# Expert tiles in a two-layer kernel: 36 instead of 39, the last eight made of two halves of different experts

## The chip, the cores and the metric

The kernel runs on one core of a Trainium2 chip. The time is device time of one execution in microseconds (us); a lower time is better. All data are float32, apart from small 0/1 tables in bfloat16. In the profile PE is TensorE (matmuls and transposes), PEld its weight loads, DVE is VectorE, ACT ScalarE, POOL GpSimd, SP SyncE; L433 is line 433 of the kernel. A float32 matmul that is no transpose shows as two records ("passes") of its row, so four matmuls are counted x8.

## What is computed

Two layers on x of shape (4, 512, 512), which is T = 2048 tokens of 512 numbers. Each layer normalises x and adds an attention and a mixture of experts to it. The first attention has 16 heads of 128 with compressed sparse and windowed local parts, the second is a plain one with 16 heads of 32. The change concerns the experts: 8 of them, and each token goes to the 2 with the highest logits.

```python
def _L0_ffn_ref(x, Wr, We, be):
    logits = jnp.einsum('bsd,de->bse', x, Wr)
    w, sel = jax.lax.top_k(logits, K_TOP)
    w = jax.nn.softmax(w, axis=-1)
    gate = jnp.einsum('bsk,bske->bse', w, jax.nn.one_hot(sel, E, dtype=w.dtype))
    for e in range(E):
        out = out + gate[..., e:e + 1] * (jnp.einsum('bsd,df->bsf', x, We[e]) + be[e])
    return out

def _L1_ffn_ref(...):
    ...
    h = jnp.einsum('td,edf->etf', xf, expert_w) + expert_b[:, None, :]
    expert_out = jax.nn.silu(h)
    combined = jnp.einsum('etf,te->tf', expert_out, full_w.reshape(-1, E)).reshape(B, S, D)
    out = jnp.einsum('bsd,df->bsf', combined, proj_w) + proj_b
    y = x + out
    rms = jnp.sqrt(jnp.mean(y * y, axis=-1, keepdims=True) + EPS)
    return norm_w * (y / rms)

xn = _layernorm(x)
x = x + _L0_attn_ref(xn, ...) + _L0_ffn_ref(xn, ...)
xn = _layernorm(x)
return x + _L1_attn_ref(xn, ...) + _L1_ffn_ref(xn, ...)
```

## The kernel before

**Layer 0's attention** runs as 32 steps (g, b): 8 groups of two heads (HG = 2), 4 sequences each. A step takes about 46 us. It projects queries, keys and values of the *next* step (`first`, `second`, `third`, `fourth`, `fifth`, L604 to L645; their matmuls are L575, and VectorE takes each product out of PSUM, L610, L631, L639), computes scores (L658, L667), turns and applies them (L693, L709 to L714, L727) and projects the result (L742). A group's weights are two blocks, `wA` and `wB`, double-buffered and loaded at the group's first step by `load_group` (L84); `combine_weights` (L107) makes four differences of them at the group's last step but one, for the next group.

**Layer 1's attention** is a walk over 64 places (g, kc): `weights` (scores of four heads, L1137, each on 32 rows of the array) and `attend` (L1151, four heads, each writing 32 columns: PSUM partitions 32 h to 32 h + 31).

**Experts.** The tokens of each expert get *slots*. Each expert's slots are rounded up to whole tiles of 128, so with 4096 token-expert pairs and 8 experts NS = 39 tiles always suffice, and all 39 are computed. Class `Routing` makes the lists. `choose` (L270) picks the two experts and counts. `place` (L306) gets the rank of each token within its expert by three small matmuls into the PSUM tile `rk` (with the triangular tables `tri` and `tri8`), and turns it into `slot` (two per token), and `wrow` (the rows of the weight array in which the weights of each tile's expert lie) by a chain of small VectorE operations (L313 to L349). `mark` and `list` (L353 to L380) invert that into `rows`, the token of each slot.

Class `Experts` (L385) handles tile i:

- `fetch_rows`, `fetch_weights`, `fetch_bias` (all through L398): indirect DMAs issued by GpSimd: the 128 token rows `xr`, the expert's weights `we` and, in layer 1, the bias `be`. In layer 0 the bias is a part of `we` (`fetch`, L413).
- `turn` (L419): four transposes on TensorE into `trm`, one copy `xT` by ScalarE (L425).
- `apply` (L428): four matmuls into `hp` (L433), bias added on VectorE (L435); in layer 1 silu (L439, L440); the tile is written to the array `yd` in DRAM by SP (L441).
- later `gather` (L443, L448) reads the two rows of each token back for 16 groups of 128 tokens.

```python
for k in range(KC):
    PE.matmul(hp, lhsT=xT[:, k, :], rhs=w[:, ts(k, HID)], start=(k == 0), stop=(k == KC - 1))
```

**The order of the work** is written out by hand: `schedule` maps places of the two attention walks to jobs. In layer 0 step 4 begins the experts, and each tile takes two places: `turn(i)`, then `apply(i)` and `fetch(i + 1)` (L840 to L844), two tiles a step, 39 tiles on 78 places from step 5 on. All buffers of the experts are single there, so tile i + 1 is fetched when tile i releases them. After the last tile `begin_combine`, then 16 combines (L847) at three places a step. From step 29 on the next layer's norms (`next_layer`, L851) are made. Layer 1's tiles lie at places `first + 4 + i * 11 // 13` (L1298), 13 tiles on 11 places; weights pass through three buffers in turn (two of a pool, and a third in a free part of `acc`), and are requested three tiles ahead, after the tile that releases the buffer. Then `begin_mixing`: gathers, `turn_mix`, `project_mix` (L1264), `finish_mix`. The engines run each its own queue in order; SP's queue issues all plain loads and stores, GpSimd's the indirect ones.

Of the kernel before, what the change touches and what calls it, by code (L numbers as in the profile page):

```python
# [29 lines left out]
E = 8  # L30
NS = 2 * T // P + E - 1
# [14 lines left out]
def two_layers(ctx: ExitStack, tc: tile.TileContext, a: dict, out: bass.AP, large: bass.AP):  # L46
# [37 lines left out]
    def load_group(g, between=None, behind=lambda: None):  # L84


        b2 = wpool.tile([P, 2, 3 * D], F32, tag="b2", name=f"b2_{g}")
        ws = []
        for i, nm in enumerate(("wA", "wB")):
            w = wpool.tile([P, KC, 3 * D], F32, tag=nm, name=f"{nm}_{g}")  # L90
            for f in range(2):
                nc.sync.dma_start(out=w[:, ts(f, 2), :],
                                  in_=a[nm][g, ts(f, 2 * P), :].rearrange("(k p) c -> p k c", p=P))
                if between:
                    between(nm, f)
            nc.sync.dma_start(out=b2[:, i, :], in_=a["b" + nm[1]][g].partition_broadcast(P))
            if i == 0:
                behind()
            ws.append(w)
        return ws, b2  # L100
# [18 lines left out]
    wk = wv = bkv = cmask = lmask = eidx = tri = tri8 = row = part = None  # L119
# [38 lines left out]
    groups = {0: load_group(0, load_between, load_tables)}  # L158
# [95 lines left out]
    class Routing:  # L254
# [4 lines left out]

        def __init__(self, name, lg, pool, out, bank):  # L260
            self.name, self.lg, self.pool, self.bank = name, lg, pool, bank
            self.gate = self.t("gate", [P, 2, NT], pool=out)
            self.slot = self.t("slot", [P, 2, NT], I32, pool=out)
            self.wrow = self.t("wrow", [P, NS], I32, pool=out)
            self.rows = self.t("rows", [P, NS], I32, pool=out)

# [39 lines left out]
        def place(self):  # L306
            flat = lambda x: x.rearrange("p n e -> p (n e)")
            rk = self.bank("sc", f"rk_{self.name}")
            PE.matmul(rk[:, 0 : NT * E], lhsT=tri, rhs=flat(self.sel), start=True, stop=False)
            PE.matmul(rk[:, 0 : NT * E], lhsT=ones_sq, rhs=flat(self.before), start=False, stop=True)  # L310
            PE.matmul(rk[:, ds(NT * E, E)], lhsT=ones_sq, rhs=self.last, start=True, stop=True)
            pos = self.t("pos", full)
            V.tensor_copy(pos, rk[:, 0 : NT * E].rearrange("p (n e) -> p n e", e=E))  # L313
            cnt = self.t("cnt", [P, E])
            V.tensor_copy(cnt, rk[:, ds(NT * E, E)])

            wide_ = [P, E, NT]
            big = self.t("big", wide_)
            V.tensor_scalar(big, row[:, 0:NT].unsqueeze(1).to_broadcast(wide_), float(P), None, ALU.mult)
            V.tensor_tensor(big, cnt.unsqueeze(2).to_broadcast(wide_), big, ALU.is_gt)  # L320
            nt = self.t("nt", [P, E])
            V.tensor_reduce(nt, big, AX.X, ALU.add)
            upto = self.t("upto", [P, E, E])
            V.tensor_tensor(upto, nt.unsqueeze(1).to_broadcast([P, E, E]), tri8, ALU.mult)
            end = self.t("end", [P, E])
            V.tensor_reduce(end, upto, AX.X, ALU.add)
            V.tensor_tensor(nt, end, nt, ALU.subtract)
            V.tensor_scalar(nt, nt, float(P), None, ALU.mult)
            V.tensor_tensor(pos, pos, nt.unsqueeze(1).to_broadcast(full), ALU.add)
            own, at = self.t("own", full), self.t("at", [P, NT])  # L330
            for k in range(2):
                V.tensor_tensor(own, self.oh[k], pos, ALU.mult)
                V.tensor_reduce(at, own, AX.X, ALU.add)
                V.tensor_copy(self.slot[:, k, :], at)
            past = self.t("past", [P, NS, E])
            V.tensor_tensor(past, row[:, 0:NS].unsqueeze(2).to_broadcast([P, NS, E]),
                            end.unsqueeze(1).to_broadcast([P, NS, E]), ALU.is_ge)
            te = self.t("te", [P, NS])
            V.tensor_reduce(te, past, AX.X, ALU.add)
            V.tensor_scalar(te, te, float(E - 1), float(P), ALU.min, ALU.mult)  # L340
            V.tensor_scalar(te, te, part[:, 0:1], None, ALU.add)
            V.tensor_copy(self.wrow, te)

            part_of = self.t("part_of", [P, 2, NT], I32)
            self.tile_f, self.row_f = self.t("tile_f", [P, 2, NT]), self.t("row_f", [P, 2, NT])
            V.tensor_scalar(part_of, self.slot, 7, None, ALU.arith_shift_right)
            V.tensor_copy(self.tile_f, part_of)
            V.tensor_scalar(part_of, self.slot, P - 1, None, ALU.bitwise_and)
            V.tensor_copy(self.row_f, part_of)  # L349
            self.sum = self.t("sum", [P, 2 * NS])  # L350
            self.pairs = {}
# [33 lines left out]
    class Experts:  # L385


        def __init__(self, r, yd, w_all, bias, third, silu, pool, bank):

            self.r, self.yd, self.w_all, self.bias, self.third = r, yd, w_all, bias, third  # L390
            self.silu, self.pool, self.bank = silu, pool, bank
            self.bufs = 2 if silu else 1
            self.w, self.x, self.b = {}, {}, {}

        def load(self, tag, i, idx, src, out=None):
            if out is None:
                out = self.pool.tile([P, src.shape[1]], F32, tag=tag, name=f"{tag}_{self.r.name}_{i}", bufs=self.bufs)
            G.indirect_dma_start(out=out, out_offset=None, in_=src, in_offset=at_rows(idx[:, i : i + 1]))  # L398
            return out

        def fetch_rows(self, i):
            if i < NS:
                self.x[i] = self.load("xr", i, self.r.rows, xnd)

        def fetch_weights(self, i):
            if i < NS:
                self.w[i] = self.load("we", i, self.r.wrow, self.w_all, self.third if i % 3 == 2 else None)

        def fetch_bias(self, i):
            if i < NS:  # L410
                self.b[i] = self.load("be", i, self.r.wrow, self.bias)

        def fetch(self, i):  # L413

            self.fetch_rows(i)
            self.fetch_weights(i)
            self.b[i] = self.w[i][:, ts(KC, HID)]
# [10 lines left out]
        def apply(self, i):  # L428
            w, xT = self.w.pop(i), self.x.pop(i)
            nm = f"{self.r.name}_{i}"  # L430
            hp = self.bank("mm", f"hp_{nm}")
            for k in range(KC):
                PE.matmul(hp, lhsT=xT[:, k, :], rhs=w[:, ts(k, HID)], start=(k == 0), stop=(k == KC - 1))  # L433
            y = self.pool.tile([P, HID], F32, tag="yr", name=f"yr_{nm}", bufs=2 if self.silu else 1)
            V.tensor_tensor(y, hp, self.b.pop(i), ALU.add)  # L435
            if self.silu:

                th = self.pool.tile([P, HID], F32, tag="th", name=f"th_{nm}")
                A.activation(th, y, AF.Tanh, scale=0.5)  # L439
                V.scalar_tensor_tensor(y, th, 1.0, y, ALU.add, ALU.mult)  # L440
            nc.sync.dma_start(out=self.yd[ts(i, P), :], in_=y)  # L441
# [324 lines left out]
    lg0, lg1 = (const.tile(full, F32, tag=f"lg_r{i}", name=f"lg_r{i}") for i in range(2))  # L766
# [41 lines left out]
    def begin_experts():  # L808
# [3 lines left out]
        rout["ex"] = Experts(rout["r"], yds[0], a["Wex"], None, None, False, rout["pool"], psum)  # L812
# [75 lines left out]
    def rest():  # L888
        nonlocal wk, wv, bkv, cmask, lmask, eidx, tri, tri8, row, part
# [17 lines left out]
        tri = load(const, "tri", [P, P], a["c_tri"])  # L907
        tri8 = load(const, "tri8", [P, E, E], a["c_tri8"])
# [26 lines left out]
    for i, (g, b) in enumerate(steps):  # L935
        if b == 0:
            if g:
                out_w[g] = load_out(g)
            if g + 1 < NH // HG:
                groups[g + 1] = load_group(g + 1)  # L940
# [7 lines left out]
        if more:  # L948
# [3 lines left out]
            sums_x()  # L952
        run0((i, 0))
# [272 lines left out]

    def begin_experts1():
        scratch.close()
        pool = scratch.enter_context(tc.tile_pool(name="moe1", bufs=1, side="right"))
        rout["ex1"] = Experts(r1, yds[1], a["ewm"], a["ebx"], acc[:, ts(3, TC), :].rearrange("p n h -> p (n h)"),  # L1230
                               True, pool, bank1)
# [66 lines left out]
    here_ = [first + 4 + i * 11 // 13 for i in range(NS)]  # L1298
# [4 lines left out]
    for i, here in enumerate(here_):  # L1303
        jobs1.append((at[here], lambda i=i: rout["ex1"].apply(i)))
        jobs1.append((at[here], lambda i=i: rout["ex1"].fetch_weights(i + 3)))
        jobs1.append((at[here], lambda i=i: rout["ex1"].fetch_bias(i + 2)))
    first += 6 + NS * 11 // 13
# [778 lines left out]
```

## Time and profile before

| | us |
|---|---|
| three timed runs, median (lowest to highest) | 2095.26 (2093.95 to 2096.58) |
| the profiled execution, own time | 2093.09 |
| its span | 2091.20 |
| time around the span | 1.89 |
| granted TensorE clock | 0.997 of full speed |

| stretch of the span, us | what runs | TensorE busy |
|---|---|---|
| 0 to 52 | loads, norms, first projection | 35.3 of 52 |
| 52 to 209 | steps 0 to 3: norms and compression beside attention | 151.7 of 157 |
| 209 to 278 | placement, marks, lists, first expert tile | 66.3 of 69 |
| 278 to 1150 | layer 0's expert tiles beside attention | 872.0 of 872 |
| 1150 to 1430 | combines and next norms beside attention | 271.8 of 280 |
| 1430 to 1560 | change of layer, placement of layer 1 | 123.5 of 130 |
| 1560 to 1880 | layer 1's expert tiles beside attention | 320.0 of 320 |
| 1880 to 2091 | mixing, projections, the end | 195.6 of 211 |

The times come from one profiled execution. Rows of TensorE overlap at their ends, so the cost of a group is the distance from its start to the next start. A group in the page gives the line, the engine, the tiles written and read, the count, then busy time and the mean of one in ns. In a timeline the columns are start, length, engine, line, operation, tiles and shapes, and in brackets how long the engine sat idle before and what released it.

### The profile page before, as it was taken

The page shows a single profiled execution, that of the slowest core. Times are in us where ns is not written, and L with a number is a line of the kernel's source. Part 1 is how long each engine was busy: PE and PEld are TensorE (multiplying, and loading weights), DVE is VectorE, ACT ScalarE, POOL GpSimd, SP SyncE. Part 2 cuts the span into 40 slices and gives each one's busy share as a digit, 9 for nine tenths or more (in the row PEclk, how much of TensorE's full clock was granted, in tenths as well). Part 3 has the DMA queues.
Part 4 walks back from the last instruction along what each step waited for, and adds up shares of the span by engine and source line. Part 5 has one row for each costly group of instructions (what it writes and reads, how often), then busy time and mean ns, then how long its engine had stood idle before and what let it go on. Part 6 is the DMA issues. An engine that isn't in the chain of part 4 may idle for free.

```text
span 2091.2 us, 27819 instructions
## 1 busy us (share of the span) xinstructions
PE 2036.2 (97%) x9074; PEld 1219.9 (58%) x9074; DVE 1456.7 (70%) x3498; ACT 873.5 (42%) x2609; POOL 743.6 (36%) x752
## 2 busy tenths in 40 slices
PE   6999999999999999999999999998999999999988
PEld 3666666666666666666666666665344445445442
DVE  7889867666666766666676777887685565556775
ACT  4554444444444444444444444544243332333332
POOL 4422244443333333333323344454114332332651
PEclk9999999999999999999999999999999999999999
DMA  8102134323433332343343222222227765663551
GB/s 266 66 31 59 44 119 140 107 96 119 142 107 114 139 109 97 117 143 107 111 142 110 72 72 72 70 92 87 91 91 237 240 222 182 229 224 126 144 162 63
DMA packets 98121, 259.26 MB, mean 124 GB/s; under 512 B 14192, under 2 KB 27504, under 8 KB 87984
## 3 DMA queue, kind: packets, MB, share of 16 engines
q0 software_dynamic: 25712, 139.48, 20.5%
q1 hardware_dynamic: 71104, 115.81, 16.5%
q10 hardware_dynamic: 1152, 2.10, 0.3%
q8 instruction: 75, 1.23, 0.2%
q14 instruction: 78, 0.64, 0.1%
HBM read 212.52 MB, written 44.30 MB: 123 GB/s over the span
## 4 chain that ended last, share of the span: by engine, by line
PE 82%; DVE 8%; POOL 3%; ACT 3%; issue 2%; DMA 1%; ACTq 0%; DVEq 0%; POOLq 0%
PE p L575 23%; PE hp_r L433 13%; PE op L742 10%; PE st L667 4%; PE st L1137 3%; PE qp L1113 3%; PE sp L658 2%; PE cx L1151 2%; PE ca L711 2%; PE trm_r L423 2%; PE qp L1097 1%; PE o L1220 1%; PE vp L1059 1%; PE trq L595 1%; PE vp L1073 1%
## 5 line engine op out<-in xcount | busy, mean ns | idle before, releaser
L433 PE MATMUL hp_r<-we_r,xT_r 128*128 128x512 f32 x520 | 234.8, 594 | 0.0
L742 PE MATMUL op<-Wo,cT 128*128 128x512 f32 x512 | 230.4, 598 | 4.5 <-DVE lv L639 3.1
L398 POOL DMA_INDIRECT xr_r<-xnd,rows_r x78 | 95.6, 1225 | 373.3 <-PE trm_r L423 333.9
L675 POOL TENSOR_TENSOR lT<-lT,lmask 128x512 f32<-128x512 f32 (+1 forms) x128 | 156.6, 1235 | 144.7 <-ACT lT L671 144.5
L575 PE MATMUL p<-wB,x 128*128 128x384 f32 x512 | 175.5, 487 | 3.2 <-DVE u L631 3.2
L575 PE MATMUL p<-wT,x 128*128 128x384 f32 x512 | 177.9, 490 | 0.5 <-DVE wT L114 0.5
L575 PE MATMUL p<-wA,xnT 128*128 128x384 f32 x512 | 173.0, 489 | 0.4 <-DVE u L610 0.4
L742 PEld LDWEIGHTS op<-Wo,cT 128*128 128x128 f32 x512 | 91.9, 190 | 114.4 <-issue 77.5
L478 ACT ACTIVATE sq<-qb 128x128 f32<-128x128 f32 x384 | 119.0, 310 | 91.4 <-DVE qb L624 44.6
L433 PEld LDWEIGHTS hp_r<-we_r,xT_r 128*128 128x128 f32 x520 | 93.7, 190 | 100.1 <-issue 94.0
L1139 ACT ACTIVATE pT<-st 128x1024 f32<-128x1024 f32 x128 | 123.9, 1014 | 62.5 <-PE st L1137 51.5
L745 DVE TENSOR_TENSOR acc<-acc,op 128x512 f32<-128x512 f32 x128 | 87.5, 686 | 69.1 <-PE op L742 68.8
L575 PEld LDWEIGHTS p<-wB,x 128*128 128x128 f32 x512 | 94.2, 190 | 66.8 <-issue 9.3
L425 ACT COPY xT_r<-trm_r 128x512 f32<-128x512 f32 x78 | 45.3, 581 | 208.6 <-PE hp_r L433 198.0
L575 PEld LDWEIGHTS p<-wT,x 128*128 128x128 f32 x512 | 94.6, 192 | 62.2 <-issue 7.1
L575 PEld LDWEIGHTS p<-wA,xnT 128*128 128x128 f32 x512 | 95.0, 192 | 60.8 <-issue 1.7
L589 ACT ACTIVATE qb<-qb,ss 128x128 f32<-128x128 f32 x256 | 81.9, 390 | 111.7 <-POOL ss L480 110.7
L671 ACT ACTIVATE lT<-st,ss 128x256 f32<-128x256 f32 (+1 forms) x128 | 46.9, 448 | 177.3 <-PE st L667 177.2
L667 PE MATMUL st<-qkT 128*128 128x256 f32 (+1 forms) x512 | 108.6, 353 | 0.0
L448 POOL DMA_INDIRECT row_r<-yd,slot_r x64 | 74.4, 1163 | 90.4 <-DVE row_r L1249 33.5
L667 PEld LDWEIGHTS st<-qkT 128*128 128x128 f32 x512 | 92.1, 191 | 10.6 <-issue 1.0
L480 POOL TENSOR_TENSOR ss<-ss,nhalf 128x6 f32<-128x6 f32 x64 | 94.9, 1483 | 5.3
(329 smaller groups left out, 4326.8 us busy)
## 6 DMA issues: line engine op xcount, KB each, us to landing
x<-xsd SPq DMA_DIRECT2D x112, 256.0 KB
yd<-yr_r SPq DMA_DIRECT2D x78, 256.0 KB
wA<-in_wA SPq DMA_DIRECT2D x16, 384.0 KB
wB<-in_wB SPq DMA_DIRECT2D x16, 384.0 KB
xnd<-xn SPq DMA_DIRECT2D x24, 256.0 KB
accd<-acc SPq DMA_DIRECT2D x18, 256.0 KB
acc<-in_x SPq DMA_DIRECT2D x16, 256.0 KB
Wo<-in_Wo SPq DMA_DIRECT2D x8, 512.0 KB
```

Source lines behind the costliest of these rows:

```text
L398: G.indirect_dma_start(out=out, out_offset=None, in_=src, in_offset=at_rows(idx[:, i : i + 1]))
L433: PE.matmul(hp, lhsT=xT[:, k, :], rhs=w[:, ts(k, HID)], start=(k == 0), stop=(k == KC - 1))
L448: G.indirect_dma_start(out=x, out_offset=None, in_=self.yd, in_offset=at_rows(self.r.slot[:, k, n : n + 1]))
L478: A.activation(sq, x[:, h, :], AF.Square, accum_out=ss[:, h : h + 1])
L480: G.tensor_tensor(ss, ss, nhalf[:, 0:n], ALU.pow)
L575: PE.matmul(p, lhsT=x[:, k, ts(c, P)], rhs=w[:, k, :], start=(k == 0), stop=(k == 1))
L589: A.activation(x[:, j, :], x[:, j, :], AF.Copy, scale=sq[t][:, j : j + 1])
L667: PE.matmul(st[:, ds((t % 2) * 256, n)], lhsT=qkT[:, HG + h, ts(t, P)], rhs=qkT[:, h, ds(t * P, n)], start=True, stop=True)
L675: G.tensor_tensor(dst, dst, lmask.rearrange("p a w j -> p (a w j)")[:, 0:n], ALU.mult)
L742: PE.matmul(op, lhsT=cT[:, h, ts(t, P)], rhs=wo[:, h, :], start=(h == 0), stop=(h == HG - 1))
L745: V.tensor_tensor(acc[:, n, :], acc[:, n, :], op, ALU.add)
L1139: A.activation(pt[:, ts(pair, 2), :], st, AF.Exp, scale=SCALE1)
```

## The change

Each expert's slots are now rounded up to halves of 128 (HALF = 64). NS becomes 36. Whole tiles come first, in order of experts. The half tiles of all experts follow, two to a tile, so the last NS − FULL = 8 tiles may have different experts in their two halves, and FULL = 28 is the number that can be taken as whole in any case. Such a tile is computed with two sets of weights by eight matmuls of 64 columns, the results lying in PSUM partitions 0 to 63 and 64 to 127.

- `place` computes numbers of whole tiles and half tiles for each expert, their starts, the shift `late` for tokens in a half tile, `wrow` with two entries for each of the last eight tiles and `brow`, the bias row of each partition in those. `tri` and `tri8` are loaded in each `Routing` and no longer once as constants.
- `Experts` has a list `sets` of weight sets (44) and of the sets that each tile owns. Layer 0 gets an extra weight buffer `we2`, filled from a new array `Wh` without the bias (one array of the host's layout of We), and the bias `bo` by `brow`. Layer 1 passes all sets through its three buffers, in order.
- Layer 0 takes tiles in order 0 to 35, on 72 places. Layer 1 takes them in `order1`, where the half tiles stand at every position with i % 9 in (3, 8), on places `first + 4 + i * 11 // 12`.
- `wA` of the attention weights has one buffer and is loaded two steps later in the group, after `first()` of the step; `lg0` and `lg1` share a buffer.

```diff
-NS = 2 * T // P + E - 1
+HALF = P // 2
+FULL = (2 * T // HALF - E) // 2
+NS = ((2 * T + E * (HALF - 1)) // HALF + 1) // 2
...
-    def load_group(g, between=None, behind=lambda: None):
...
+    def load_block(g, nm, between=None):
+        w = wpool.tile([P, KC, 3 * D], F32, tag=nm, name=f"{nm}_{g}", bufs=1 if nm == "wA" else 2)
+        for f in range(2):
+            nc.sync.dma_start(out=w[:, ts(f, 2), :],
+                              in_=a[nm][g, ts(f, 2 * P), :].rearrange("(k p) c -> p k c", p=P))
...
+    def load_later(g):
+        w = load_block(g, "wB")
+        b2 = wpool.tile([P, 2, 3 * D], F32, tag="b2", name=f"b2_{g}")
+        for i, nm in enumerate(("bA", "bB")):
+            nc.sync.dma_start(out=b2[:, i, :], in_=a[nm][g].partition_broadcast(P))
+        return [[None, w], b2]
...
         def place(self):
...
+            V.tensor_tensor(cmp, cnt.unsqueeze(2).to_broadcast(wide_), big, ALU.is_gt)
+            V.tensor_reduce(half, cmp, AX.X, ALU.add)
+            V.tensor_scalar(big, big, float(HALF), None, ALU.add)
+            V.tensor_tensor(cmp, cnt.unsqueeze(2).to_broadcast(wide_), big, ALU.is_gt)
+            V.tensor_reduce(whole, cmp, AX.X, ALU.add)
+            V.tensor_tensor(half, half, whole, ALU.subtract)
...
+            V.tensor_tensor(late, pos, much.unsqueeze(1).to_broadcast(full), ALU.is_ge)
+            V.tensor_tensor(late, late, more.unsqueeze(1).to_broadcast(full), ALU.mult)
+            V.tensor_tensor(pos, pos, start.unsqueeze(1).to_broadcast(full), ALU.add)
+            V.tensor_tensor(pos, pos, late, ALU.add)
...
         def fetch(self, i):
             self.fetch_rows(i)
-            self.fetch_weights(i)
-            self.b[i] = self.w[i][:, ts(KC, HID)]
+            for h, j in enumerate(self.own[i]):
+                n = self.sets[j]
+                self.w[j] = self.load(("we", "we2")[h], j, self.r.wrow[:, n : n + 1], (self.w_all, self.halves)[h])
+            if len(self.own[i]) == 1:
+                self.b[i] = self.w[self.own[i][0]][:, ts(KC, HID)]
+            else:
+                n = self.order[i] - FULL
+                self.b[i] = self.load("bo", i, self.r.brow[:, n : n + 1], self.bias)
...
         def apply(self, i):
-            w, xT = self.w.pop(i), self.x.pop(i)
+            ws, xT = [self.w.pop(j) for j in self.own[i]], self.x.pop(i)
+            n, m = self.order[i], P // len(ws)
...
             for k in range(KC):
-                PE.matmul(hp, lhsT=xT[:, k, :], rhs=w[:, ts(k, HID)], start=(k == 0), stop=(k == KC - 1))
+                for h, w in enumerate(ws):
+                    PE.matmul(hp[ts(h, m), :], lhsT=xT[:, k, ts(h, m)], rhs=w[:, ts(k, HID)],
+                              start=(k == 0), stop=(k == KC - 1))
...
-                groups[g + 1] = load_group(g + 1)
+                groups[g + 1] = load_later(g + 1)
...
             first()
             sums_x()
+            if b == 2 and g + 1 in groups:
+                groups[g + 1][0][0] = load_block(g + 1, "wA")
...
+    order1, whole_, halves_ = [], list(range(FULL)), list(range(FULL, NS))
+    for i in range(NS):
+        order1.append((halves_ if i % 9 in (3, 8) else whole_).pop(0))
...
-    here_ = [first + 4 + i * 11 // 13 for i in range(NS)]
+    here_ = [first + 4 + i * 11 // 12 for i in range(NS)]
...
-        jobs1.append((at[here], lambda i=i: rout["ex1"].apply(i)))
-        jobs1.append((at[here], lambda i=i: rout["ex1"].fetch_weights(i + 3)))
-        jobs1.append((at[here], lambda i=i: rout["ex1"].fetch_bias(i + 2)))
-    first += 6 + NS * 11 // 13
+        def after(i=i):
+            ex = rout["ex1"]
+            ex.apply(i)
+            for j in ex.own[i]:
+                ex.fetch_weights(j + 3)
+            ex.fetch_bias(i + 2)
+        jobs1.append((at[here], after))
+    first += 6 + NS * 11 // 12
```

The rest of `place` (starts of the halves, their experts, `wrow` and `brow`) is more small VectorE operations of the same shapes, 128 partitions by 1 to 128 elements; in all about 25 more than before in each layer.

## The prediction

> **What bounds the kernel now.** I read the page's busy shares first, then its chain of waits, then the busy time in chosen stretches, the groups with their forms apart, and last the timelines around the experts' tiles and the placement. The page, with the chain that ended last:
>
> ```profile
> PE 2036.2 (97%) x9074; PEld 1219.9 (58%) x9074; DVE 1456.7 (70%) x3498; ACT 873.5 (42%) x2609; POOL 743.6 (36%) x752
> ...
> PE 82%; DVE 8%; POOL 3%; ACT 3%; issue 2%; DMA 1%; ACTq 0%; DVEq 0%; POOLq 0%
> ```
>
> TensorE is busy 97% of the span and makes 82% of the chain. What a shorter TensorE stream is worth depends on the stage, so I cut out the stretches in which tiles run (columns: window; busy PE, PEld, DVE, ACT, POOL; clock; DMA share; GB/s):
>
> ```profile
> 627.00:836.00 209.00, 209.00 (x915) 136.25 (x914) 141.66 (x377) 90.66 (x316) 68.52 (x65) 1.00 0.33 114
> 1046.00:1255.00 209.00, 207.19 (x934) 137.41 (x933) 149.77 (x404) 94.29 (x336) 75.70 (x72) 1.00 0.30 98
> 1560.00:1880.00 320.00, 320.00 (x1338) 149.44 (x1336) 181.20 (x248) 113.69 (x168) 111.56 (x112) 1.00 0.67 223
> ```
>
> In both layers' tile stretches TensorE has no gap at all, VectorE is below 72%, the DMA engines at a third (layer 0) and two thirds (layer 1). A tile less is therefore its whole TensorE time less. What one tile costs stands in TensorE's timeline, in layer 0 and in layer 1 (start, length, row; successive starts give the cost, since ends overlap):
>
> ```profile
> 832.03 0.60 PE L423 MATMUL trm_r<-ident,xr_r 128*128 128x128 f32 x4
> 832.47 1.06 PE L658 MATMUL sp<-ckT,qkT 128*128 128x32 f32 x8
> ...
> 835.21 3.60 PE L433 MATMUL hp_r<-we_r,xT_r 128*128 128x512 f32 x8
> 838.64 2.74 PE L575 MATMUL p<-wT,x 128*128 128x384 f32 x8
> ```
>
> ```profile
> 1710.50 0.60 PE L423 MATMUL trm_r<-ident,xr_r 128*128 128x128 f32 x4
> 1710.94 3.60 PE L433 MATMUL hp_r<-we_r,xT_r 128*128 128x512 f32 x8
> 1714.47 1.14 PE L1137 MATMUL st<-qk 32*128 32x512 f32 x8
> 1715.54 1.05 PE L1151 MATMUL cx<-pT,v 128*32 128x512 f32 x6
> ```
>
> Four f32 matmuls show as 8 passes, 838.64 − 835.21 = 3.43 us, 429 ns a pass. The transposes take 0.44 us. A whole tile: 3.87 us.
>
> **What the skill says.** (1) The Trainium skill, "TensorEngine Tiling (Array Packing)", Tiling Modes, lists 128×64 as a mode of two tiles, says that tiles "operate independently", and that changing the mode drains the engine. No 64-column matmul runs before, but the attention of layer 1 writes four 32-column groups: the rows show 8 passes (four matmuls) of L1151 from 1705.95 to the next start at 1706.94, 0.99 us, where four matmuls one after another would take 8 × 0.429 = 3.43. So column tiles do overlap for f32 operands with four different moving tensors. The drain: hp followed by the 32-row st takes 1714.47 − 1710.94 = 3.53 us against 3.43, so about 0.09 us a change. (2) "TensorE: Matmul & The Clock Gate", Part 3, gives a pack's span as one matmul plus about 4 ns for each further tile; in the raw records here the four passes start 6 to 7 ns apart. (3) "VectorE: DVE Perf Modes", the section on the TRN2 errata, says that small operations pay a fixed cost; here 128x8 rows take 0.16 to 0.17 us. (4) "DMA: Bandwidth & Descriptors", Anatomy of one DMA, fits 2.0 us plus bytes/436 GB/s; the 1.31 MB `we` would be 5.0, the trace shows 6.1 to 7.5, and I use the trace.
>
> **The change, part by part.**
>
> *Tiles removed.* Three a layer, 6 × 3.87 = −23.2 us of TensorE, all in stretches that are full. Their copies, bias adds, silu and stores lie on engines with room: nothing.
>
> *Half tiles.* Sixteen tiles now do eight matmuls of 64 columns, 16 passes in 8 pairs. If a pair runs together at 429 to 436 ns, 8 × 436 = 3.49, +0.06 us a tile. The change of mode adds 0.09 on entering and 0.09 on leaving. In layer 0 both are new; in layer 1 one edge was a change already (hp to st). 8 × (0.06 + 0.18) + 8 × (0.06 + 0.09) = +3.1 us. Bounds: no drain at all and perfect pairs +1; pairs as slow as the L1151 groups (0.495 us for each round) 16 × 8 × 0.066 = +8.4. I take the middle row because a pair has half as many weight loads to place as a group of four, and those are 108 ns each (L1151's PEld), 432 of the 495.
>
> *Placement.* About 25 more small VectorE operations per layer, one after another: by the 128x8, 128x64 and 128x128 rows (0.16, 0.22, 0.29 us, issued 0.10 to 0.30 apart) 4 to 5 us of VectorE per layer. Layer 0 runs them among steps where TensorE is already held by VectorE's evacuations:
>
> ```profile
> 218.16 0.19 DVE L721 RECIPROCAL sums<-sums 128x8 f32<-128x8 f32 x1
> 218.28 0.17 DVE L327 TENSOR_TENSOR nt_r<-end_r,nt_r 128x8 f32<-128x8 f32 x1
> 218.37 0.48 DVE L336 TENSOR_TENSOR past_r<-row,end_r 128x312 f32<-128x312 f32 x1
> ```
>
> ```profile
> 223.61 1.56 PE L575 MATMUL p<-wB,x 128*128 128x384 f32 x4 [0.99 <-DVE u L631]
> ```
>
> VectorE had 19.12 of 23 us busy there (209 to 232), so little cover: the context row of L727 and the `u` evacuations of L631 queue behind the chain. I take +2 in layer 0 (0 if the new operations only fill VectorE's 3.9 free microseconds, +5 if all is exposed). In layer 1 (1510 to 1516) VectorE is 52.95 of 60 busy but TensorE 59.84 of 60: three PSUM buffers cover some; L1061, the evacuation of values, waits in the chain; +1.5 (0 to 5). Rows for the first tile are due about 9 us before they are needed. Together +3.5, bounds 0 to 10.
>
> *Weights of half tiles.* Layer 0's second set and bias go into buffers of their own, issued by POOL behind `we`, at the preceding apply. POOL takes 1.1 us for each issue. Issue to use of `we` alternates between about 11 us (issued 839.82, used 852.94: 13.1 with the issue itself) and 20. `we` takes 6.1 to 7.5; 1.05 MB more at the rate seen adds about 4 and the bias 1 (layer 1's 0.26 MB lands 1 us behind its set): 10.4 to 11.4. It is tight in the four half tiles that have the short lead, where TensorE's queue (next step's projections) would stand behind L433: +0.7 (0 to 6). Layer 1: sets rotate through three buffers, requested a tile or more ahead, at least 9 us against 6 plus 4 for a pair's second set, and 223 GB/s rises to about 247 inside half tiles: nothing, as long as the DMA engines have that third free; without it up to 0.5 us a half tile, +4.
>
> *The attention weights.* One buffer of wA instead of two. The load of the next group now waits for the current group's last `first()`, but the trace shows that before's second buffer was released at the same point one group later: before issues wA at 511.79, it lands by 516.1, and the same slot's first reader, the fourth subtraction of L114, starts at 533.13. In the new program that issue serves this very reader: 17 us of slack, nothing. The wB halves and biases stay ahead of it on SP's queue, as do the sums' loads; all are short (0.3 to 0.9 us of issue). tri and tri8 are issued by SP some 29 us before place() in layer 0, and in layer 1 at its start, long before 1507: nothing; if SP were held by their release they would stand in front of the rows' writes, at most 2 us.
>
> *Moved work.* Layer 0's combine begins 6 slots earlier (step 22 instead of 24) and ends a step earlier, and the next layer's norms (step 29 on) no longer share VectorE with it. TensorE's gaps there are 1.8 us at 1373.9 (released by the norm's `xn`) and 1.0 at 1382.4: −1.0 (0 to −2). In layer 1 tiles take the same 33 places, 11 for 12 rather than for 13, so mixing begins where it did; its gathers' waits (the chain's row_r pieces of 3.3 to 4.5 us) stay.
>
> **Sum.** −23.2 + 3.1 + 3.5 + 0.7 − 1.0 = −16.9. The profiled execution took 2093.09 us (span 2091.20 and 1.89 around it), so 2076.2. The median of the runs, 2095.26, lies 2.17 above it: 2078.4, say 2078.
>
> **Rivals.** (B) *Given back by VectorE and late weights*: placement at 8, half tiles' sets 5, pairs 8: −23.2 + 21 = −2 to −9, 2086 to 2093. For it: VectorE's 83% at 209 to 232. Against it: an average gap there is 1 us, and the layer-0 lead is 20 us every other tile. (C) *Halves one after another*: 16 passes × 0.429 = 6.86 us, +3.43 a tile, 16 × 3.43 = +54.9; with the changes of mode (16 × 0.09 + 8 × 0.09 = 2.2), placement, weights and combine as above −23.2 + 54.9 + 2.2 + 3.5 + 0.7 − 1.0 = +37.1, so 2132, slower. It decides as soon as a pair of passes costs over 0.57 us: 128 pairs have (23.2 − 5.4)/128 = 0.14 to spend above 0.43. For it: no matmul of 64 columns and 128 rows is in the trace. Against it: L1151's four groups read different moving tensors too, in 0.99 us. (D) *More*: placement hidden, combine worth 2: −23.2 + 1 to 2 − 2 = −24, 2071. (E) *Doesn't do what it says*: 36 tiles need that the half rests fit 8 tiles; their number is fixed by the program, not by data, and each owner's sets are all loaded, so only the split between whole and half tiles changes; time is the same.
>
> **Chances.** Forecast (2072 to 2085) 0.75, B 0.10, C 0.09, D 0.04, other slower cases 0.02. Range 2069 to 2091: it holds the forecast, D and most of B. A measurement of this kernel can tell about 0.2% (4.2 us) from no change, so faster means below 2091: 0.75 + 0.04 + most of B = 0.87; same 0.02; slower 0.11.
>
> **What would show it.** L433 in 704 records (2 × 28 × 8 whole, 16 × 16 of 64 columns) where there are 624 now; in half tiles the next row starts 3.5 to 3.7 us after L433 (forecast) or 6.9 (C). TensorE still full in 627 to 836 and 1560 to 1880. Gaps on TensorE at 215 to 230 and around 1512 growing by 2 each (placement), waits of hp on `we2` or `bo` above 1 us (weights), a wait of L114 on wA (attention weights). I am wrong if the pairs show as serial, or if layer 1's tile stretch opens gaps on DMA.

## The result, and the profile after

The changed kernel takes 2073.68 us (median of four runs, 2073.40 to 2074.66), the kernel before 2094.94 in the same comparison: ratio 0.9899, 95% interval 0.9881 to 0.9916, 21.3 us faster. The forecast was 2078, range 2069 to 2091. The profiled execution took 2074.66 us, its span 2072.6; from profile to profile the gain is 18.4 us.

Busy shares and chain of the changed kernel's page:

```profile
PE 2017.7 (97%) x9130; PEld 1205.3 (58%) x9130; DVE 1452.0 (70%) x3543; ACT 867.9 (42%) x2600; POOL 754.3 (36%) x761
...
PE 81%; DVE 8%; ACT 3%; POOL 2%; DMA 2%; issue 1%; SPq 0%; ACTq 0%; POOLq 0%; DVEq 0%
```

The nature of the bound is the same: TensorE, 97%. Its busy time fell by 18.5 us (2036.2 to 2017.7), which is the fall of the span (18.6): what went is work of TensorE, and almost nothing of it came back as idle time. The tile stretches stay full (same columns as in the forecast's windows; 278 to 1150 is layer 0's stretch, and the 1.24 us missing there lie at 1133 and 1139, behind its last tile):

```profile
278.00:1150.00 872.00, 870.76 (x3906) 565.38 (x3905) 588.49 (x1560) 381.76 (x1333) 328.10 (x306) 1.00 0.37 127
1560.00:1880.00 320.00, 319.70 (x1424) 149.05 (x1424) 186.62 (x258) 115.01 (x169) 108.56 (x108) 1.00 0.69 234
```

A half tile in TensorE's timeline of layer 0, and below it the rows around the whole tile of the kernel before, whose own two rows the prediction shows:

```profile
929.79 0.49 PE L779 MATMUL trs<-ident,s 128*128 128x128 f32 x3
930.21 3.65 PE L518 MATMUL hp_r<-we_r,xT_r 128*64 128x512 f32 x16
933.80 2.85 PE L661 MATMUL p<-wT,x 128*128 128x384 f32 x8
936.48 0.60 PE L681 MATMUL trq<-ident,qb 128*128 128x128 f32 x4
```

```profile
834.88 0.49 PE L693 MATMUL trs<-ident,s 128*128 128x128 f32 x3
...
841.22 0.60 PE L595 MATMUL trq<-ident,qb 128*128 128x128 f32 x4
```

Sixteen passes in 3.59 us: the two halves run beside each other. The whole tile of the kernel before needed 3.43 for eight. The rest of the price lies at the edges. Before, the three transposes ahead of the tile took 0.33 us to the tile's start (834.88 to 835.21), here 0.42; the projections behind it took 2.58 to the next row (838.64 to 841.22), here 2.68. So 0.09 + 0.16 + 0.10 = 0.35 us a half tile.

The single records behind these rows say where the 0.35 goes. A *change of mode*, here and below, is a change of how many rows or columns of the array the matmuls of TensorE use. The last transpose ahead of the half tile takes 0.203 us to the next start instead of 0.109, and the first pair then 0.480 instead of 0.429; the later pairs keep to 0.429. On leaving, the last pair takes 0.523 instead of 0.429, and the first pass of the projections 0.426 instead of 0.322. A change therefore shows on both sides: about 0.09 us before the first pass of the new mode starts, and 0.05 to 0.10 us in that pass. The pairs themselves cost nothing.

Since starts on TensorE can be matched between two traces, the gain can be booked by stretch. The table is worked out from the starts of TensorE's rows; "again" is a second profile of the changed kernel (e9).

| from | to | before | changed | again |
|---|---|---|---|---|
| start | scores of step 3 | 191.4 | 193.3 | 192.4 |
| step 3 | first expert tile | 94.5 | 95.9 | 96.0 |
| first tile | step 19 | 629.7 | 629.7 | 629.7 |
| step 19 | step 23 (eight half tiles) | 183.1 | 185.9 | 185.9 |
| step 23 | first context of layer 1 | 396.6 | 384.6 | 385.7 |
| first context | first projection of the mixing | 437.1 | 422.6 | 422.2 |
| that | last row | 149.1 | 150.6 | 150.1 |

The stretch from the first tile to step 19 agrees to 0.01 us between all profiles of this study, so that differences of 0.1 us can be read in a stretch where TensorE is full. The first and the last row vary: over thirteen profiles of related kernels they took 191.0 to 195.6 and 149.1 to 150.9. Kernels built on the one before had 191.4 to 192.7 in the first, those built on the changed one 191.0 to 195.6. Whether about 1 us of that is the change's own stays open. In the first profile these two rows are 3.4 us longer than before, which is why the gain from profile to profile, 18.4 us, is smaller than that of the medians. The five rows between give 1.4 + 0 + 2.8 − 12.0 − 14.5 = −22.3 us for the first profile and −21.6 for the second, close to the medians' 21.3.

The row that had not been foreseen is the one of layer 1. Three tiles at 3.87 are 11.6, and half tiles and placement should have given back 1.5 to 3 there, yet it fell by 14.5. In the kernel before, a place that holds two tiles reads so:

```profile
1610.16 1.07 PE L1151 MATMUL cx<-pT,v 128*32 128x512 f32 x8
1611.16 1.09 PE L423 MATMUL trm_r<-ident,xr_r 128*128 128x128 f32 x8
1612.09 3.60 PE L433 MATMUL hp_r<-we_r,xT_r 128*128 128x512 f32 x8
1615.62 1.12 PE L1137 MATMUL st<-qk 32*128 32x512 f32 x2
1616.67 3.70 PE L433 MATMUL hp_r<-we_r,xT_r 128*128 128x512 f32 x8
1620.30 1.14 PE L1137 MATMUL st<-qk 32*128 32x512 f32 x6
1621.36 1.07 PE L1151 MATMUL cx<-pT,v 128*32 128x512 f32 x8
```

and in the changed kernel, with one tile there:

```profile
1605.44 1.06 PE L1238 MATMUL cx<-pT,v 128*32 128x512 f32 x8
1606.43 0.66 PE L506 MATMUL trm_r<-ident,xr_r 128*128 128x128 f32 x4
1606.93 3.60 PE L518 MATMUL hp_r<-we_r,xT_r 128*128 128x512 f32 x8
1610.46 1.14 PE L1224 MATMUL st<-qk 32*128 32x512 f32 x8
1611.53 1.07 PE L1238 MATMUL cx<-pT,v 128*32 128x512 f32 x8
```

Four score matmuls, each on 32 rows, run beside each other: 1.07 us for all eight passes (1610.46 to 1611.53). Before, the compiled order puts one of them ahead of the second tile and three behind it. The lone one takes 1.05 us, the three 1.06: a split costs a whole round. At a place with two tiles the lone matmul has a reason in the program: the turned rows `xT` have one buffer, so the second tile's copy waits for the first tile's matmuls. In e11 below, where `xT` has two and this tile stays in its place, this split is gone. From context to context the place went from 11.20 to 6.09 us, 5.1 for one tile. The kernel before has 16 such splits by an expert tile, ten of them at its six places with two tiles, the changed one 12, five of them at its three such places. Why the compiled order splits the others, at places with one tile, stays open. From the first context to the mixing the score matmuls take 71.4 us before and 67.6 after (67.2 in the second profile). So about 4 of the 14.5 us are four splits fewer.

### The profile page after: what moved, and what is told of

Its sections match the earlier page's. It is cut to its first block, busy times and chain, and to the rows that moved or that the text cites. A ratio compares the mean times of both kernels' runs of the same rounds, so it can differ in the third digit from the quotient of the medians.

```text
span 2072.6 us, 27984 instructions
## 1 busy us (share of the span) xinstructions
PE 2017.7 (97%) x9130; PEld 1205.3 (58%) x9130; DVE 1452.0 (70%) x3543; ACT 867.9 (42%) x2600; POOL 754.3 (36%) x761
## 4 chain that ended last, share of the span: by engine, by line
PE 81%; DVE 8%; ACT 3%; POOL 2%; DMA 2%; issue 1%; SPq 0%; ACTq 0%; POOLq 0%; DVEq 0%
PE p L661 23%; PE hp_r L518 12%; PE op L828 10%; PE st L753 4%; PE st L1224 3%; PE qp L1200 3%; PE sp L744 3%; PE cx L1238 2%; PE ca L797 2%; PE o L1307 2%; PE trm_r L506 2%; PE vp L1160 1%; PE trq L681 1%; PE trk L687 1%; PE cc L800 1%
## 5 line engine op out<-in xcount | busy, mean ns | idle before, releaser
L518 PE MATMUL hp_r<-we_r,xT_r 128*128 128x512 f32 (+1 forms) x592 | 224.8, 596 | 0.0
L470 POOL DMA_INDIRECT xr_r<-xnd,rows_r x72 | 89.4, 1242 | 331.6 <-PE trm_r L506 298.2
L518 PEld LDWEIGHTS hp_r<-we_r,xT_r 128*128 128x128 f32 (+1 forms) x592 | 83.8, 170 | 97.3 <-issue 91.8
L661 PEld LDWEIGHTS p<-wT,x 128*128 128x128 f32 x512 | 94.5, 193 | 63.5 <-issue 6.7
```

What stands on the lines that cost most here:

```text
L518: PE.matmul(hp[ts(h, m), :], lhsT=xT[:, k, ts(h, m)], rhs=w[:, ts(k, HID)], start=(k == 0), stop=(k == KC - 1))
L661: PE.matmul(p, lhsT=x[:, k, ts(c, P)], rhs=w[:, k, :], start=(k == 0), stop=(k == 1))
```

## The experiments

The runs lie on several chips; each ratio is to the kernel before on the same chip.

**e1: the halves in turn.**

```diff
-            for k in range(KC):
-                for h, w in enumerate(ws):
+            for h, w in enumerate(ws):
+                for k in range(KC):
```

> The changed kernel, with the eight matmuls of a half tile ordered half by half (four of the left half, then four of the right) instead of the two halves alternating. Theory: the halves run beside each other only because neighbours in TensorE's queue belong to different halves; in turn, each half tile takes 16 passes of 0.43 us, 6.9 us instead of 3.6, and the kernel 16 x 3.3 = 53 us more, about 2127. Rival: TensorE pairs them whatever the order in its queue, about 2074.

Measured 2101.88 us (ratio 1.0036, 1.0023 to 1.0049): 28 us more than the changed kernel, half of what the theory said, and slower than before. TensorE's timeline of this kernel:

```profile
948.44 5.42 PE L518 MATMUL hp_r<-we_r,xT_r 128*64 128x512 f32 x16
953.79 2.52 PE L661 MATMUL p<-wB,x 128*128 128x384 f32 x7
```

From the half tile's start to the next row's (whose last pass lies outside this view) it takes 5.35 us instead of 3.59. In the records of another half tile the right half's first pass starts at 930.371, together with the left half's fifth of eight (930.365): four passes alone, four pairs, four alone, twelve rounds of 0.43 instead of eight. 16 × 4 × 0.43 = 27.5, close to the 28 measured. Both theories missed: some of the pairs form even so, but not all. Whether TensorE brings the right half forward or the compiled order of its queue does, the records don't tell. The case in which the change makes the kernel slower was near: the order of two loops is enough.

**e2 and e3: the tile behind the next place's four score matmuls**, in the changed kernel and in the one before.

```diff
-        jobs1.append((at[here], after))
+        jobs1.append((at[here], lambda f=after: deferred.append(f)))
...
             nxt = weights(g, kc)
+            for f in deferred:
+                f()
+            deferred.clear()
```

> The changed kernel, but in layer 1 an expert tile's matmuls are placed behind the next place's four score matmuls, so that they no longer stand between the first score matmul and the other three. Theory: the compiled order splits these four at 12 places (1 and 3 instead of 4), each split costs the time of a row-packed round, about 1.1 us, because the lone matmul takes as long as four together: 12 x 1.1 = 13 us less, about 2061. Rival: the lone score matmul only fills a wait for the tile's transposed rows, and TensorE would stand idle there: no change, about 2074.

> The same edit in the kernel before, where 16 groups of score matmuls are split. Theory: 16 x 1.1 = 18 us less, about 2077.5; then the change is worth only about 16.5 us once no group is split in either kernel, because 4 of its 21 us are four splits fewer. Rival: no change (2095), and the change's extra 4 us come from somewhere else.

Measured: e2 2069.72 us (0.9878, 0.9862 to 0.9895), e3 2091.67 (0.9985, 0.9978 to 0.9991). Splits by expert tiles are all but gone in both, and yet e3 gained only about 3.5 us. e2's median is 4.0 below the changed kernel's, but the two intervals overlap, and in the stretch that the edit touches only 1.0 us went. TensorE's time by kind, from the first context of layer 1 to the mixing (us, start to next start, idle time included):

| | before | e3 | changed | e2 |
|---|---|---|---|---|
| all | 437.1 | 433.2 | 422.6 | 421.6 |
| score matmuls | 71.4 | 56.9 | 67.6 | 58.0 |
| experts' matmuls | 139.2 | 141.6 | 128.7 | 132.4 |
| context matmuls | 48.7 | 52.8 | 48.7 | 50.8 |
| experts' transposes | 18.7 | 20.9 | 17.8 | 19.9 |
| sums of keys | 11.7 | 13.3 | 11.7 | 12.5 |

Most of what the splits cost left the score matmuls, 14.5 and 9.6 us of the 18 and 13 expected. But now the tile stands between scores and contexts in 33 places, and each neighbour pays for the change of mode, as in these rows of e2; and some context groups are split instead, by three tiles in e2 and six in e3:

```profile
1608.14 0.66 PE L506 MATMUL trm_r<-ident,xr_r 128*128 128x128 f32 x4
1608.73 1.14 PE L1224 MATMUL st<-qk 32*128 32x512 f32 x8
1609.80 3.70 PE L518 MATMUL hp_r<-we_r,xT_r 128*128 128x512 f32 x8
1613.43 1.06 PE L1238 MATMUL cx<-pT,v 128*32 128x512 f32 x8
```

The transposes take 0.59 to the next start instead of 0.50, the tile 3.63 instead of 3.53. All this gives 8.7 us back in e2, 10.6 in e3. The part of the theory about its size for the whole kernel fell. The part about the change is not settled by these two: in the stretch, profile to profile, the kernels differ by 11.5 us instead of 14.5, as the theory has it, but the medians differ by 22.0, where it had 16.5.

**e4: score matmuls kept in program order.**

```diff
-                PE.matmul(st[:, i, :], ...)
+                tc.keep_in_program_order(PE.matmul(st[:, i, :], ...))
```

> The changed kernel, but each score matmul of layer 1 is kept behind everything that the program has before it on TensorE, expert tiles included, so that all 64 groups of four are whole and stand behind the expert tile instead of before it. Theory: 13 us less as well, minus what TensorE waits for the transposed rows (about 1 us at a tile that is turned just before): 2061 to 2072. Rival: the waits take all of it, 2074 or more.

Measured 2074.49 us (0.9897, 0.9881 to 0.9914): no gain. All 64 groups of scores are whole (54.7 us instead of 67.6), but the contexts take 60.7 instead of 48.7. Neither theory has that. The rival has the right time by the wrong way, for TensorE hardly waits more than in the changed kernel (1.2 us idle in the stretch against 0.9). With the scores whole their 12 splits are priced, 67.6 − 54.7 = 12.9 us, close to the 13 expected for e2. Its timeline:

```profile
1604.61 1.04 PE L1238 MATMUL cx<-pT,v 128*32 128x512 f32 x2
1605.59 3.70 PE L518 MATMUL hp_r<-we_r,xT_r 128*128 128x512 f32 x8
1609.22 1.14 PE L1224 MATMUL st<-qk 32*128 32x512 f32 x8
1610.29 1.06 PE L1238 MATMUL cx<-pT,v 128*32 128x512 f32 x6
```

The compiled order has put one context matmul where a score matmul stood. The contexts are a packed group too, of four times 32 columns, and the lone one takes 0.98 us, as long as four (0.99 in the changed kernel). The expert tile splits nine such groups (the timeline has nine rows of x2 ahead of a tile).

**e5: half tiles with one set.**

```diff
-                cols = [n] if n < FULL else [FULL + 2 * (n - FULL) + h for h in range(2)]
+                cols = [n] if n < FULL else [FULL + 2 * (n - FULL)]
```

> The changed kernel, but each of the last eight tiles is computed with the first of its two sets of weights alone, four matmuls of 128 columns; the products of the right halves with their own expert's weights are left out (36 whole tiles, no second set, no extra bias load). Theory (a half tile costs over a whole one only its changes of mode and 6 ns a pair): the trace of the changed kernel has 2.8 us for the eight half tiles of layer 0 and about 1 for those of layer 1, so 3.8 us less, about 2070. Rival (late second sets hold TensorE in layer 0, or the added DMA slows layer 1): 6 to 10 us less, 2064 to 2068.

Measured 2070.04 us (0.9876, 0.9859 to 0.9892), 3.6 below the changed kernel's median on another chip, with intervals that overlap; it is the trace that decides. There step 19 to step 23 takes 183.1 again, all of the 2.8 us; in layer 1 the experts' tiles, from the first to the mixing, take 347.5 instead of 348.6. Together 3.9 us, 0.35 for a half tile in layer 0 and 0.14 in layer 1, and in layer 0 all of it is at the edges shown above. Nothing is left for late weights: in these steps of the changed kernel TensorE has no gap at all.

**e6: a longer placement in the kernel before.**

```diff
             V.tensor_reduce(nt, big, AX.X, ALU.add)
+            for _ in range(18):
+                V.tensor_scalar(nt, nt, 1.0, None, ALU.mult)
...
+            for _ in range(9):
+                V.tensor_scalar(pos, pos, 1.0, None, ALU.mult)
```

> The kernel before with 27 more small operations in the chain of place() in each layer (18 of 128x8, 9 of 128x128, multiplications by one), all of them in the chain that the slots wait for. Theory: what the longer chain costs is what it delays of VectorE's evacuations: the changed kernel shows 1.3 us between the ranks and the first tile in layer 0 and 0.5 to 0.9 in layer 1, so 1.5 to 2.5 us more, about 2097. Rival (as the forecast had it): 3.5 us more, 2098.5; other rival: the whole chain is exposed twice, 8 to 10 us more, 2104.

Measured 2102.52 us (1.0029, 1.0018 to 1.0039), 6.8 us more: more than theory and forecast, less than the chain exposed twice. In layer 0 step 3 to the first tile is 1.3 us longer, as in the changed kernel (1.4). In layer 1 the first context to the first tile is 4.6 us longer, where the changed kernel is 0.6 to 0.9 longer. Another 1.7 us lie ahead of that, between step 23 and the first context, where nothing was added; their cause stays open. This experiment puts all 27 operations in one chain; in the change, which also has 27 more in the lines of `place`, many lie beside it. e6's gaps on TensorE in layer 1 (behind the bracket: idle time and releaser):

```profile
1536.23 2.04 PE L1141 MATMUL st<-qk 32*128 32x512 f32 x8 [1.62 <-ACT pT L1143]
...
1541.15 3.70 PE L1063 MATMUL vp<-wvT,xnT 128*128 128x512 f32 x8 [1.49 <-DVE sum_r L380]
```

and the changed kernel's:

```profile
1527.21 3.70 PE L1146 MATMUL vp<-wvT,xnT 128*128 128x512 f32 x8 [0.44 <-DVE sum_r L439]
```

The values wait for a bank that the lists (`sum_r`) give back late. The chain from the copied ranks to the last `slot`, read from VectorE's timeline in layers 0 and 1, takes 7.9 and 5.0 us before, 9.4 and 7.4 in the changed kernel, 19.6 and 11.2 in e6. So e6 is the longer chain by far, and its number of operations is a poor price. Nor is the chain's length one: 11.8 us more in layer 0 cost 1.3, 6.2 more in layer 1 cost 4.6. What TensorE has to wait for behind the chain must be read in each place.

**e7: one buffer of wA in the kernel before**, loaded as in the change.

```diff
+        w = wpool.tile([P, KC, 3 * D], F32, tag=nm, name=f"{nm}_{g}", bufs=1 if nm == "wA" else 2)
...
+            if b == 2 and g + 1 in groups:
+                groups[g + 1][0][0] = load_block(g + 1, "wA")
```

> The kernel before with one buffer for wA, loaded behind the last reading of the group, as in the changed kernel. Theory: 17 us of slack before its first reader, no change (2095, within 1). Rival: the load is late or crosses with others at the group's end, up to 1 us in each of seven groups, 2098 to 2102; in the traces it would be a wait of VectorE's differences on wA.

Measured 2096.91 us, ratio 1.0004 (0.9996 to 1.0013): no difference that can be told. First tile to step 19 takes 629.7 us, as ever.

**e8 to e11: a better order, in both kernels.** Two buffers for `xT` in layer 1, and fewer tiles moved behind the four scores: in e8 those of the second place of each group (nine places, behind eight of which the scores were split), in e10 those of places with two tiles too.

```diff
-            xT = self.pool.tile([P, KC, P], F32, tag="xT", name=f"xT_{self.r.name}_{i}")
+            xT = self.pool.tile([P, KC, P], F32, tag="xT", name=f"xT_{self.r.name}_{i}", bufs=self.bufs)
...
-        jobs1.append((at[here], after))
+        jobs1.append((at[here], (lambda f=after: deferred.append(f)) if at[here][1] == 1 else after))
```

> The changed kernel with two buffers for the turned rows in layer 1, and with the tiles of the places after which the score matmuls were split placed behind these four (eight places). Theory: the whole edit of e2 moved all 33 places and gave back in changes of mode what it saved in splits; moved at eight places alone, 8 x (1.05 - 0.27) = 6.2 us, and two buffers save three splits more, 3.4: 9.6 us less, about 2064. Rival: what TensorE waited for (a free PSUM bank, the turned rows) comes back as idle time: 2069 to 2073.

> The changed kernel as it is, on the same chip and with the same runs of the kernel before as the next two. Expected 21 us below before (ratio 0.9899 again). What its profile is for: the stretch up to step 3 and the one behind the first projection of the mixing differ by up to 4.6 and 1.8 us between profiles of one program; if the 1.9 and 1.6 us that the first profile of the changed kernel was longer there belong to the change, they show again; if not, the value lies anywhere in 191.0 to 195.6 and 149.0 to 150.9.

> e8 with the places that have two tiles behind their score matmuls too, so that one group of scores is split before the mixing (at the first tile) where e8 has two and the changed kernel 12. Theory: from the first context of layer 1 to the mixing 415.5 us in e8, one split less minus a change of mode gives 414.6 to 415.2, so 7.5 us below the changed kernel, about 2066. Rival (waits of the row buffers): 415.5 or more, no gain over e8.

> e8's edit in the kernel before (with one buffer shared by the two layers' logits, as in the change, to make room), splits 16 before and 4 now. Theory: 10 us from the splits, about 2085, and the stretch from the first context to the mixing 437.1 -> 427: the change is then worth 11 to 12 us in that stretch (three tiles less, half tiles more) instead of 14.5, since the rest of it were splits. Rival (the change's extra has nothing to do with the splits): it stays 14.5 between this kernel and e8, 430.

| | us | ratio to before | first context to mixing, us | of it scores |
|---|---|---|---|---|
| e8 | 2068.21 | 0.9863 (0.9846 to 0.9879) | 415.5 | 57.0 |
| e9, changed | 2074.20 | 0.9904 (0.9888 to 0.9919) | 422.2 | 67.2 |
| e10 | 2064.56 | 0.9851 (0.9836 to 0.9866) | 413.5 | 56.0 |
| e11, before with e8's edit | 2084.22 | 0.9950 (0.9936 to 0.9964) | 425.8 | 58.8 |

e8 gained 7.1 us in its stretch instead of 9.6: scores fell by 10.5, tiles and transposes gave back 3.4. Of these, 2.6 are two waits of TensorE, for `xr_r` (1.60) and `we_r` (1.01), so e8's rival was right in part. e10, beyond its forecast, is 9.6 us faster than the changed kernel on the same chip and beats both kernels. Its timeline, where a tile that had split the scores now stands behind them while the next place keeps the cheaper order:

```profile
1599.66 0.60 PE L506 MATMUL trm_r<-ident,xr_r 128*128 128x128 f32 x4
1600.19 1.14 PE L1224 MATMUL st<-qk 32*128 32x512 f32 x8
1601.26 3.70 PE L518 MATMUL hp_r<-we_r,xT_r 128*128 128x512 f32 x8
1604.89 1.07 PE L1238 MATMUL cx<-pT,v 128*32 128x512 f32 x8
1605.89 0.66 PE L506 MATMUL trm_r<-ident,xr_r 128*128 128x128 f32 x4
1606.38 3.60 PE L518 MATMUL hp_r<-we_r,xT_r 128*128 128x512 f32 x8
1609.91 1.14 PE L1224 MATMUL st<-qk 32*128 32x512 f32 x8
```

e11 agrees with the booking but does not prove it: with most splits out of both kernels, the change is worth 425.8 − 415.5 = 10.4 us in this stretch instead of 14.5. But e11 has still four splits by tiles to e8's two (1.8 us in the scores), and e8 has 2.0 us more idle time than e11, so that the fall by 4.1 is not the splits alone. What prices them is the score row itself, 71.4 against 67.6 and 67.2. e9 settled the first and last stretch of the table no further: 192.4 and 150.1 lie inside the range of the others.

## Why the prediction was right, and by how much it missed

The direction, the mechanism and the range held; the gain was 21.3 us where 16.9 had been summed. From profile to profile it was 18.4, nearer to the sum, but that is chance: a gain of about 4 us that the sum lacked stands against 3.4 us in the first and last stretch, which vary from profile to profile anyway. Of the signs that the forecast named, most came: L518 has 704 records, the row behind a half tile starts 3.59 us after it, and no wait on `we2` or `bo` shows. Idle time of TensorE around the placement grew by 1.0 us in layer 0 and 0.5 to 0.8 in layer 1, not by 2 each.

- *Six tiles, −23.2*: right in layer 0 (396.6 to 384.6 or 385.7, where three tiles at 3.87 are 11.6, with nothing else of size in that stretch). In layer 1 a tile was under-sized. It was priced from the row of the tile and its transposes alone. That it also splits the scores was in the same timeline, as a row of x2 ahead of a tile and one of x6 behind it, and the forecast had not asked what a tile does to its neighbours. Four splits fewer: about 4 us (3.8 and 4.2 in the score rows of the two profiles), the term that was missing.
- *Half tiles, +3.1, and late weights, +0.7*: their sum, 3.8, agrees with the 3.9 measured (2.8 and 1.1) by luck. A half tile in layer 0 costs 0.35 instead of 0.24: the forecast counted the 0.09 us ahead of each change of mode, but not the slower first pass behind it, and it counted 0.06 for the pairs, which cost nothing. Against that, no second set came late.
- *Placement, +3.5*: 1.4 in layer 0 and 0.9 or less in layer 1. The forecast took the operations as one after another, 4 to 5 us a layer; the chain to the slots grew by 1.5 and 2.4 us. e6 shows that about 6 us (1.3 + 4.6) would have been possible with as many operations, all in the chain.
- *One buffer of wA, 0*: right, e7.
- *Combine and norms, −1.0*: at most 0.4 of the fall by 12.0 in the first profile, and the second shows none (10.9). The TensorE gaps that this step counted on are of the size of what varies there.
- *Profile against median, 2.2*: the profiled execution of the kernel before was below its median, that of the changed one 1.0 above. Neither is the change's.
- *Rival C, halves one after another*: did not come, but e1 shows that it hung on the order of the loops. Even in that order its full price (+54.9) did not come, but 28.

## What to carry to other kernels

Where TensorE is full, price a removed piece by the distance between its neighbours, not by its own rows: it may break up a group of small matmuls that run beside each other, and a lone member takes as long as the whole group. Interleave the members of a packed group in the program, and keep foreign matmuls out of it, and look in the trace for what the compiled order made of it; but count the changes of mode that the new order makes, about 0.1 us for each neighbour, and the waits that the old order covered. Where an engine is never idle, two traces of it can be subtracted row by row, which tells effects of 0.1 us that medians with 2 us between runs can't; stretches with idle time, like the first and the last here, vary by more.

## What the runs showed of the hardware

- Two matmuls of 64 columns and 128 rows with different moving tensors run beside each other in float32: passes of the pair start 6 ns apart, pairs every 0.43 us, the rate of one matmul of 128 columns (changed kernel, layer 0).
- With the program ordered half by half, the right half starts with the left half's fifth pass: half of the passes overlap, 5.35 us instead of 3.59 (e1).
- From start to the next row's start, a matmul of 32 rows alone takes 1.05 us (before), four on different rows 1.07 (changed); one of 32 columns alone 0.98 (e4), four 0.99 (changed).
- A change of mode costs about 0.09 us before the first pass of the new mode starts (0.203 instead of 0.109, 0.523 instead of 0.429), and 0.05 to 0.10 us in that pass (0.480 instead of 0.429, 0.426 instead of 0.322). A 64-column tile among 128-column matmuls pays both at both edges, 0.35 us.
